# Weight sums on GpSimd, statistics in odd units and aggregation in quarters, in a two-layer window-attention and convolution kernel

## The chip, the cores and the metric

The kernel runs on one core of one Trainium2 chip. The metric is the device time of one execution in microseconds (us). Engines are named as in the profile: PE is TensorE's matmuls and PEld its weight loads, DVE is VectorE, ACT is ScalarE, POOL is GpSimd, SP is SyncE, which here issues most DMAs.

## The reference: what is computed

The input `x` is 2 images of 128 channels, 256 by 256, in float32. Two residual layers follow each other, and each first normalises its input over groups of 4 channels and a whole image:

```python
def _gn(v, G=32, eps=1e-5):
    g = v.reshape(B_, G, C_ // G, H_, W_)
    m = jnp.mean(g, axis=(2, 3, 4), keepdims=True)
    s = jnp.var(g, axis=(2, 3, 4), keepdims=True)
    return ((g - m) / jnp.sqrt(s + eps)).reshape(v.shape)
...
x = x + _L0_conv_ref(_gn(x), L0_conv_W_qkv, L0_conv_W_out, L0_conv_rel_height, L0_conv_rel_width)
x = x + _L1_conv_ref(_gn(x), L1_conv_w1, L1_conv_w3, L1_conv_w4)
```

Layer 0 is attention in windows of 8 by 8 pixels with a halo (keys from 12 by 12), 4 heads of 32, a relative position bias and a fixed mask that keeps one parity of rows and columns. Layer 1 multiplies two branches: a vertical 5-tap convolution over all channels followed by a 3-tap depthwise one, and a horizontal 3-tap product with dilation 2 into 8 channels.

What matters here is the normalisation. The mean and variance of a group need every row of the image first. So statistics of image 0 of `x` stand ahead of everything; those of image 1 of `x`, and those of layer 0's results (`y0`, `y1` in the code's names), can be gathered on the way.

## The kernel before, in words

**Work and its order.** Layer 0 handles an image in 32 strips of 8 rows, and each strip in two units (row parity `r`). Units count from 0 to 127: unit `u` is strip `k = u // 2`, parity `u % 2`; image 1 begins at unit 64. Layer 1 handles 64 strips. Inside both layers the order of instructions on every engine is the order in which the code is written (`tc.manual_schedule`); each engine works through its own queue in that order and waits on semaphores. The setup stands outside of that block.

**Setup (L220 to L247).** Image 0 comes in 32 tiles of 8 rows (`f_sx`, six buffers, L246). Each tile gets four `bn_stats` of 512 elements (L117, called by `chunk`, L115 to L119), which leave 6 numbers each in a tile of 128 × 6 = 768 per partition. Then `Norms.steps` (L121 to L158) makes mean and 1/deviation: a `bn_aggr` over the 768 (L125), a small matmul that averages over the 4 channels of a group (L128), four small DVE operations (L131 to L136), a second small matmul (L139), and a chain through ACT's square root (L142 to L156). The pool of the raw rows (`f_raw`) lies over the setup's buffers, so its first load (L283) starts when the last statistics are done.

**A unit of layer 0 (the loop at L544).** In the order of the code, and with the engines:

1. In even units: `load_rows(k + 2)` (SP, L283), then `normalise(k + 1)`: a POOL copy (L308), four DVE operations (L317) and two DVE copies (L322, L323).
2. If the unit is in `stats_at`: the next image's statistics, four `bn_stats` from the single buffer `f_sx` (DVE, L117), then the issue of the next such load (SP, L272).
3. In unit 8 alone: `weights.sums()` (L606 to L612), six DVE operations of 128x128 that prepare layer 1's weights `w1s`.
4. POOL copies (`by_place`, L331; `old_keys`, L342), which need `normalise`.
5. Matmuls of biases (L443) and scores (L459), exponentials on ACT (L468), matmuls of values (L424), whose results ACT and DVE copy out of PSUM half and half (L430).
6. Coefficients of the next strip: matmul L403, copies L412 (ACT) and L416 (DVE). Attention matmuls L484, with DVE's L490 and L491; DVE's transposes L502.
7. Queries and keys of the next unit (L349, L384, L359); statistics of the result of unit u − 1 (L117); projection (L349) and the residual sum on DVE (L518), and the store (SP, L522).

The PSUM pool `pj`, of four banks, is used in turn by L424, L403, L484, L349 and the small matmuls of `steps`, so a late copy on DVE holds up the matmul that comes four tiles later.

`stats_at` in the kernel before has units 1, 3, ..., 59 with strips 0 to 29 of image 1, and units 4 and 8 with the last two strips. `norm_at` starts the steps for `x1` in unit 61 and for `y0` in unit 69; one step is taken at each `step()` in the unit. Layer 1 takes the steps for `y1` in its strips 3 to 7 (L857); its DVE work in a strip is L691, L695, L763, L770, L776, L788 and L809, its matmuls are L704, L723, L759 and L799.

Of the kernel before, what the change touches and what calls it, by code (L numbers as in the profile page):

```python
# [19 lines left out]
P = 128  # L20
W = 256
# [83 lines left out]
class Norms:  # L105


    def __init__(self, nc, glob, small, gavg, ns):
        self.nc, self.glob, self.small, self.gavg, self.ns = nc, glob, small, gavg, ns
        self.done = {}  # L110

    def new(self, name, tag):
        return self.glob.tile([P, self.ns * 4, 6], F32, tag=tag, name=name)
# [1 line left out]
    def chunk(self, st, n, t):  # L115
        for c in range(t.shape[1] // 2):
            self.nc.vector.bn_stats(  # L117
                st[:, n + c, :], t[:, 2 * c : 2 * c + 2, :].rearrange("p a w -> p (a w)")
            )  # L119

    def steps(self, st, ps_pool, name, tag="pj"):  # L121

        nc, glob, small, gavg = self.nc, self.glob, self.small, self.gavg
        mv = small.tile([P, 2], F32, tag="mv", name=f"mv_{name}")
        nc.vector.bn_aggr(mv, st.rearrange("p n k -> p (n k)"))  # L125
        yield
        pm = ps_pool.tile([P, 512], F32, tag=tag, name=f"pm_{name}")
        nc.tensor.matmul(pm[:, 0:1], gavg, mv[:, 0:1], start=True, stop=True)  # L128
        yield
        mean = glob.tile([P, 1], F32, tag=f"mean_{name}", name=f"mean_{name}")  # L130
        nc.vector.tensor_copy(mean, pm[:, 0:1])  # L131
        d = small.tile([P, 1], F32, tag="d", name=f"d_{name}")
        nc.vector.tensor_sub(d, mv[:, 0:1], mean)
        q = small.tile([P, 1], F32, tag="q", name=f"q_{name}")
        nc.vector.tensor_mul(q, d, d)
        nc.vector.tensor_add(q, q, mv[:, 1:2])  # L136
        yield
        pv = ps_pool.tile([P, 512], F32, tag=tag, name=f"pv_{name}")
        nc.tensor.matmul(pv[:, 0:1], gavg, q, start=True, stop=True)  # L139
        yield  # L140
        v = small.tile([P, 1], F32, tag="v", name=f"v_{name}")
        nc.vector.tensor_scalar(v, pv[:, 0:1], 1e-5, None, ALU.add)  # L142
        yield
        sd = small.tile([P, 1], F32, tag="sd", name=f"sd_{name}")
        nc.scalar.activation(sd, v, AF.Sqrt)
        yield

        r0 = small.tile([P, 1], F32, tag="r0", name=f"r0_{name}")
        nc.vector.reciprocal(r0, sd)
# [16 lines left out]
def attention_fast(tc, io, x1_d, norm, st_x, st_y, tags, ends, weights):  # L166

    nc = tc.nc
    x = io["x"]
    NB, _, H, _ = x.shape  # L170
    NS = H // 8
    NU = 2 * NB * NS
    with ExitStack() as l0:
# [45 lines left out]
        with ExitStack() as setup:  # L219
            sp = setup.enter_context(tc.tile_pool(name="f_setup", bufs=6))  # L220


            wq_nat = sp.tile([P, P], F32, tag="wq_nat", name="f_wq_nat", bufs=1)
            nc.sync.dma_start(wq_nat, io["w_q"])
            relT = sp.tile([P, 2 * NREL], F32, tag="relT", name="f_relT", bufs=1)
            nc.sync.dma_start(relT, io["relT"])
            g_rel = sp.tile([P, HEADS, 2 * NREL], F32, tag="g_rel", name="f_g_rel", bufs=1)
            for h in range(HEADS):
                pg = ps_pj.tile([P, 512], F32, tag="pj", name=f"f_pg_{h}")


                nc.tensor.matmul(
                    pg[:, : 2 * NREL], wq_nat[32 * h : 32 * h + 32, :],
                    relT[32 * h : 32 * h + 32, :], start=True, stop=True,
                )
                nc.scalar.mul(g_rel[:, h, :], pg[:, : 2 * NREL], SCALE)
            for t in range(4):
                o = 11 - 2 * t
                for t1 in range(4):
                    nc.scalar.copy(wb[:, t, t1, :, 0:6], g_rel[:, :, o : o + 11 : 2])  # L240
                o = NREL + 11 - 2 * t
                for t2 in range(4):
                    nc.scalar.copy(wb[:, t2, t, :, 6:12], g_rel[:, :, o : o + 11 : 2])
            for s in range(NS):
                t = sp.tile([P, 8, W], F32, tag="sx", name=f"f_sx_0_{s}")
                nc.sync.dma_start(t, x[0, :, 8 * s : 8 * s + 8, :])  # L246
                norm.chunk(st_x[0], 4 * s, t)  # L247

        rawp = l0.enter_context(tc.tile_pool(name="f_raw", bufs=3))
        x1p = l0.enter_context(tc.tile_pool(name="f_x1", bufs=2))  # L250
# [4 lines left out]


        stats_at, norm_at = {}, {}
        for b in range(NB - 1):
            for s in range(NS - 2):
                stats_at[2 * (b * NS + s) + 1] = b + 1, s  # L260
            stats_at[2 * (b * NS + 2)] = b + 1, NS - 1
            stats_at[2 * (b * NS + 4)] = b + 1, NS - 2
            norm_at[2 * (b * NS + NS - 2) + 1] = st_x, b + 1, f"x{b + 1}"
            norm_at[2 * ((b + 1) * NS + 2) + 1] = st_y, b, f"y{b}"
        coming, sxs = sorted(stats_at), {}

        def load_next():
            if coming:
                u = coming.pop(0)
                b, s = stats_at[u]  # L270
                sxs[u] = t = rawp.tile([P, 8, W], F32, tag="sx", name=f"f_sx_{b}_{s}", bufs=1)
                nc.sync.dma_start(t, x[b, :, 8 * s : 8 * s + 8, :])  # L272

        def input_stats(u):
            b, s = stats_at[u]
            norm.chunk(st_x[b], 4 * s, sxs.pop(u))

        def load_rows(k):

            b, s = divmod(k, NS)  # L280
            t = rawp.tile([P, 10, W], F32, tag="raw", name=f"f_raw_{k}")
            n = min(10, H - 8 * s)
            nc.sync.dma_start(t[:, 0:n, :], x[b, :, 8 * s : 8 * s + n, :])  # L283
            raws[k] = t
# [245 lines left out]
        def emit(parts):  # L530
            for f in parts:
                f()

        load_rows(0)
        load_rows(1)
        load_next()
        weights.load()
        with tc.manual_schedule(engines=ORDERED):
            normalise(0)
            by_place(0, range(4))  # L540
            emit(queries(0) + keys(0))
            coefficients(0, 0)
            coefficients(0, 1)
            for u in range(NU):  # L544
                k, r = divmod(u, 2)
                b, s = divmod(k, NS)
                later, more = u + 1 < NU, k + 1 < NB * NS
                if r == 0:
                    if k + 2 < NB * NS:
                        load_rows(k + 2)  # L550
                    if more:
                        normalise(k + 1)
                if u in stats_at:
# [24 lines left out]
                turn(u)  # L578
                step()
                if later:  # L580
                    emit(queries(u + 1) + keys(u + 1))
                step()
                if u > 0:
                    result_stats(u - 1)
                project(u)
                step()
                del qs[u]
            result_stats(NU - 1)


class Weights:
# [14 lines left out]
    def sums(self):  # L606

        w = [self.w1[:, i] for i in range(5)]
        self.nc.vector.tensor_add(self.w1s[:, 0], w[1], w[3])
        self.nc.vector.tensor_scalar(self.w1s[:, 1], w[3], -1.0, None, ALU.mult)  # L610
        for i, (a, b) in enumerate(((2, 1), (4, 3), (0, 1), (2, 3))):
            self.nc.vector.tensor_sub(self.w1s[:, 2 + i], w[a], w[b])  # L612


def convolutions_fast(tc, io, x1_d, norm, st_y, out, weights, count_good):
# [859 lines left out]
```

## Time and profile before

| What | us |
|---|---|
| median of 3 runs | 3109.14 (3107.81 to 3111.26) |
| span of the profiled execution | 3104.3 |
| the median above that span | 4.8 |
| PE busy in the span | 2971.1 |
| DVE busy in the span | 2533.3 |
| DVE: one `bn_aggr` of 768 | 3.61 |
| DVE: one `bn_stats` of 512 | 0.68 (four in a row 2.46) |
| a plain unit of layer 0 | 15.47 |

How to read the profile: it is one execution. A row of a timeline is start, duration, engine, line, operation, tiles out<-in with their shape, how many were merged, and in brackets how long the engine idled before and what ended that. A row of the stretches is the stretch and its length, then busy time and instructions of PE, PEld, DVE, ACT and POOL, the granted share of TensorE's clock, the DMA engines' busy share, and GB/s. Idle time of an engine that is not the bottleneck costs nothing. Times of different rows may overlap a little, because a DVE instruction starts before the last one's record ends.

### The profile page before, as it was taken

What the parts mean: (1) busy time and instruction counts of PE and PEld (TensorE: products, weight loads), DVE (VectorE), ACT (ScalarE), POOL (GpSimd) and SP (SyncE); (2) the same over time, 40 slices, a digit from 0 to 9 for tenths busy, and PEclk for the clock granted to TensorE, in tenths of its full rate; (3) what the DMA queues carried; (4) which work ended last, traced back from release to release, by engine and by line L of the source; (5) the groups of instructions that cost most, each with busy time, mean ns of one, the idle gap of its engine ahead of it and who ended that gap; (6) DMA issues with size and microseconds to landing.
All of it is one profiled execution on the core that took longest, in us unless ns stands there. A gap on an engine that the chain in (4) does not pass through costs nothing.

```text
span 3104.3 us, 116029 instructions
## 1 busy us (share of the span) xinstructions
PE 2971.1 (96%) x52006; PEld 2248.5 (72%) x52006; DVE 2533.3 (82%) x4092; ACT 1711.4 (55%) x2673; POOL 569.0 (18%) x921
## 2 busy tenths in 40 slices
PE   0799999999999999999999999998999999999998
PEld 0688888888888888888888888884444444444443
DVE  8788888888888878777777777767999999999998
ACT  0455555555555555555555555555666665666664
POOL 2222222222222222222222222210000000000001
PEclk9999999999999999999999999999999999999999
DMA  9433333333333222222222222215788888888886
GB/s 395 160 125 128 111 115 111 115 112 115 111 115 112 84 71 87 72 86 72 88 71 87 71 88 71 84 37 168 206 217 213 221 216 213 222 215 214 217 217 167
DMA packets 137401, 434.75 MB, mean 140 GB/s; under 512 B 12993, under 2 KB 87617, under 8 KB 104385
## 3 DMA queue, kind: packets, MB, share of 16 engines
q1 hardware_dynamic: 127824, 361.18, 34.1%
q0 software_dynamic: 9072, 66.06, 11.5%
q8 instruction: 412, 6.75, 0.9%
q14 instruction: 93, 0.75, 0.1%
HBM read 284.59 MB, written 134.22 MB: 135 GB/s over the span
## 4 chain that ended last, share of the span: by engine, by line
PE 92%; DVE 2%; issue 1%; DMA 1%; ACT 0%; POOL 0%; SPq 0%; DVEq 0%; POOLq 0%; ACTq 0%
PE f_pv L424 15%; PE a_e L723 10%; PE a_o L723 10%; PE f_pq L349 9%; PE f_s L459 8%; PE f_o L484 8%; PE f_pk L349 7%; PE f_py L349 7%; PE f_pa L403 4%; PE f_s L443 4%; PE a_d L759 3%; PE b L799 2%; PE a_c L723 2%; PE g L704 2%; DVE t L788 0%
## 5 line engine op out<-in xcount | busy, mean ns | idle before, releaser
L430 DVE COPY f_vt<-f_pv 64x512 f32<-64x512 f32 x512 | 354.6, 695 | 290.7 <-ACT f_vt L430 290.5
L424 PE MATMUL f_pv<-f_wqkvT,f_xn 128*128 128x128 f32 x4096 | 491.3, 278 | 0.0
L468 ACT ACTIVATE f_p<-f_s 128x512 f32<-128x512 f32 x512 | 264.3, 603 | 404.1 <-PE f_s L459 404.1
L384 ACT ACTIVATE f_q<-f_pq,f_head 128x512 f32<-128x512 f32 x512 | 309.9, 687 | 303.0 <-PE f_pq L349 303.0
L424 PEld LDWEIGHTS f_pv<-f_wqkvT,f_xn 128*128 128x128 f32 x4096 | 466.9, 192 | 8.6
L331 POOL COPY f_xq<-f_xn 128x256 f32<-128x256 f32 x512 | 309.9, 649 | 757.9 <-DVE f_xn L317 757.9
L430 ACT COPY f_vt<-f_pv 64x512 f32<-64x512 f32 x512 | 297.4, 582 | 118.0 <-PE f_pv L424 117.8
L781 ACT ACTIVATE t<-t,w 128x1024 f32<-128x1024 f32 x128 | 147.0, 1149 | 375.2 <-DVE t L776 369.5
L788 DVE SCALAR_TENSOR_TENSOR t<-t,w,t 128x1024 f32<-128x1024 f32 x256 | 329.8, 1288 | 7.4 <-ACT t L781 1.3
L459 PEld LDWEIGHTS f_s<-f_q,f_kt 64*64 64x64 f32 x16384 | 250.6, 135 | 49.2 <-issue 49.2
L349 PE MATMUL f_pq<-f_xn,f_wq_s 128*128 128x192 f32 (+2 forms) x1520 | 277.0, 329 | 3.3 <-DVE f_xn L317 2.5
L459 PE MATMUL f_s<-f_q,f_kt 64*64 64x64 f32 x16384 | 268.1, 220 | 0.0
L484 PE MATMUL f_o<-f_vt,f_p 128*32 128x66 f32 x16384 | 264.2, 222 | 0.8 <-DVE mean_x L131 0.3
L484 PEld LDWEIGHTS f_o<-f_vt,f_p 128*32 128x32 f32 x16384 | 242.4, 110 | 10.4 <-DVE f_cf L416 1.0
L349 PE MATMUL f_pk<-f_xn,f_wqkvT 128*128 128x256 f32 x1024 | 245.2, 380 | 0.0
L349 PEld LDWEIGHTS f_pq<-f_xn,f_wq_s 128*128 128x128 f32 x1520 | 232.3, 188 | 16.9 <-issue 4.2
L349 PE MATMUL f_py<-f_ot,f_woT 128*128 128x256 f32 x1024 | 241.7, 378 | 2.3 <-DVE f_ot L502 2.3
L723 PE MATMUL a_e<-xm,w1s 128*128 128x512 f32 x512 | 240.7, 591 | 0.0
L723 PE MATMUL a_o<-xm,w1s 128*128 128x512 f32 x512 | 240.5, 590 | 0.2 <-ACT both L754 0.2
L308 POOL COPY f_xn<-f_xn 128x1280 f32<-128x1280 f32 x62 | 86.4, 1394 | 770.8 <-PE f_pv L424 770.8
L817 POOL DMA_DIRECT2D y<-f_x x63 | 54.5, 866 | 925.1 <-DVE y L809 910.1
L518 DVE TENSOR_TENSOR f_x<-f_py,f_raw 128x512 f32<-128x512 f32 x256 | 176.0, 688 | 57.9 <-PE f_py L349 50.2
(131 smaller groups left out, 4674.7 us busy)
## 6 DMA issues: line engine op xcount, KB each, us to landing
f_raw<-in_x SPq DMA_DIRECT2D x62, 1280.0 KB, 7.5
f_sx<-in_x SPq DMA_DIRECT2D x64, 1024.0 KB, 12.4
f_x<-f_x SPq DMA_DIRECT2D x128, 512.0 KB, 3.3
y<-f_x POOLq DMA_DIRECT2D x63, 1024.0 KB, 7.9
out<-y SPq DMA_DIRECT2D x63, 1024.0 KB, 4.0
raw<-f_x SPq DMA_DIRECT2D x64, 640.0 KB, 6.4
raw<-f_x SPq DMA_DIRECT2D x62, 384.0 KB, 7.7
t<-t4p SPq DMA_DIRECT2D x192, 32.0 KB, 4.3
```

The source lines that it names most:

```text
L331: nc.gpsimd.tensor_copy(xq[:, t2, half].rearrange("p t r n c e -> p r t (n c) e"), cells[:, :, 16 * half : 16 * half + 16, 1 + t2 : 9 : 4, ...
L349: nc.tensor.matmul(dst[:, 32 * lo : 32 * hi], w, moving[:, lo:hi], start=True, stop=True)
L384: nc.scalar.activation(q[:, c, :, i], pq.rearrange("p (n x) -> p n x", n=NPAIR), AF.Copy, scale=head[:, i : i + 1],)
L424: nc.tensor.matmul(pv[:, P * n : P * n + P], xn[k % 2][:, r, 4 * j + n].rearrange("p c x -> p (c x)"), wvT, start=True, stop=True,)
L430: (nc.vector.tensor_copy if c else nc.scalar.copy)(vt[rows, 4 * j : 4 * j + 4, :, c, 0:32], pv[rows].rearrange("p (n h d) -> p n h d", n=4 ...
L459: nc.tensor.matmul(sc[g][n // 8][64 * c : 64 * c + 64, n % 8].rearrange("p i x -> p (i x)"), keys_k[rows, c, 48 * n : 48 * n + 64], qs[u][ ...
L468: nc.scalar.activation(pts[u][:, g, 8 * half : 8 * half + 8].rearrange("p n i x -> p (n i x)"), sc[g][half].rearrange("p n i x -> p (n i x ...
L484: nc.tensor.matmul(po[32 * h : 32 * h + 32, n - lo], p[:, h // 2, n, h % 2], vt[:, n, h], start=True, stop=True,)
L518: nc.vector.tensor_tensor(x1[:, :, c:W:2], py.rearrange("p (m t) -> p t m", t=4), raws[k][:, r:8:2, c:W:2], ALU.add,)
L723: nc.tensor.matmul(pa[:, : n * W], w, rows, start=i == 0, stop=i == len(terms) - 1)
L781: nc.scalar.activation(t3[:, j : j + 4], t1[:, j : j + 4, :], AF.Copy, scale=w3[:, 0:1])
L788: nc.vector.scalar_tensor_tensor(t3[:, j : j + 4], t1[:, j + tap : j + tap + 4, :], w3[:, tap : tap + 1], t3[:, j : j + 4], ALU.mult, ALU.add,
```

## The change

Four edits:

- The six operations of `weights.sums()` are issued on GpSimd instead of VectorE, still in unit 8.
- Image 1's statistics are gathered in odd units only, 1 to 59. The first eight of these (1 to 15) take ten rows, five `bn_stats`, the other 22 take eight rows; units 4 and 8 have none. The buffer and the loads of the first eight grow to ten rows.
- Aggregation goes in quarters: `quarter()` runs a `bn_aggr` over 192 numbers. Three quarters are issued on the way: in setup after tiles 7, 15 and 23; at the end of units 30, 46 and 58 for `x1`; 34, 50 and 66 for `y0`; 98, 106 and 114 for `y1`. `steps` begins with the fourth.
- `steps` joins the four quarters: the first small matmul has 4 columns instead of 1, and the DVE operations between the two small matmuls are six instead of four. The mean over quarters becomes a sum and a factor 0.25.

The diff, with the unchanged lines between left out:

```diff
+    def quarter(self, st, name, i):
+        if i == 0:
+            self.mvs[name] = self.glob.tile([P, 4, 2], F32, tag=f"mv_{name}", name=f"mv_{name}")
+        self.nc.vector.bn_aggr(
+            self.mvs[name][:, i], st[:, self.ns * i : self.ns * i + self.ns].rearrange("p n k -> p (n k)")
+        )
...
-        mv = small.tile([P, 2], F32, tag="mv", name=f"mv_{name}")
-        nc.vector.bn_aggr(mv, st.rearrange("p n k -> p (n k)"))
+        self.quarter(st, name, 3)
+        mv = self.mvs[name]
...
-        nc.tensor.matmul(pm[:, 0:1], gavg, mv[:, 0:1], start=True, stop=True)
+        nc.tensor.matmul(pm[:, 0:4], gavg, mv[:, :, 0], start=True, stop=True)
...
-        nc.vector.tensor_copy(mean, pm[:, 0:1])
-        d = small.tile([P, 1], F32, tag="d", name=f"d_{name}")
-        nc.vector.tensor_sub(d, mv[:, 0:1], mean)
+        nc.vector.tensor_reduce(mean, pm[:, 0:4], AX.X, ALU.add)
+        nc.vector.tensor_scalar(mean, mean, 0.25, None, ALU.mult)
+        d = small.tile([P, 4], F32, tag="d", name=f"d_{name}")
+        nc.vector.tensor_scalar(d, mv[:, :, 0], mean, None, ALU.subtract)
+        nc.vector.tensor_mul(d, d, d)
+        nc.vector.tensor_add(d, d, mv[:, :, 1])
         q = small.tile([P, 1], F32, tag="q", name=f"q_{name}")
-        nc.vector.tensor_mul(q, d, d)
-        nc.vector.tensor_add(q, q, mv[:, 1:2])
+        nc.vector.tensor_reduce(q, d, AX.X, ALU.add)
...
-        nc.vector.tensor_scalar(v, pv[:, 0:1], 1e-5, None, ALU.add)
+        nc.vector.tensor_scalar(v, pv[:, 0:1], 0.25, 1e-5, ALU.mult, ALU.add)
...
                 norm.chunk(st_x[0], 4 * s, t)
+                if s % 8 == 7 and s < 31:
+                    norm.quarter(st_x[0], "x0", s // 8)
...
-            for s in range(NS - 2):
-                stats_at[2 * (b * NS + s) + 1] = b + 1, s
-            stats_at[2 * (b * NS + 2)] = b + 1, NS - 1
-            stats_at[2 * (b * NS + 4)] = b + 1, NS - 2
+            row = 0
+            for i in range(NS - 2):
+                n = 10 if i < 8 else 8
+                stats_at[2 * (b * NS + i) + 1] = b + 1, row, n
+                row += n
+            for i, u in enumerate((30, 46, 58)):
+                quarter_at[2 * b * NS + u] = st_x, b + 1, f"x{b + 1}", i
...
+        for b in range(NB):
+            for i, u in enumerate((34, 50, 66) if b + 1 < NB else (34, 42, 50)):
+                quarter_at[2 * b * NS + u] = st_y, b, f"y{b}", i
...
-                sxs[u] = t = rawp.tile([P, 8, W], F32, tag="sx", name=f"f_sx_{b}_{s}", bufs=1)
-                nc.sync.dma_start(t, x[b, :, 8 * s : 8 * s + 8, :])
+                t = rawp.tile([P, 10, W], F32, tag="sx", name=f"f_sx_{b}_{row}", bufs=1)
+                sxs[u] = t[:, 0:n]
+                nc.sync.dma_start(sxs[u], x[b, :, row : row + n, :])
...
                 project(u)
                 step()
+                if u in quarter_at:
+                    st, i, name, part = quarter_at[u]
+                    norm.quarter(st[i], name, part)
...
-        self.nc.vector.tensor_add(self.w1s[:, 0], w[1], w[3])
-        self.nc.vector.tensor_scalar(self.w1s[:, 1], w[3], -1.0, None, ALU.mult)
+        self.nc.gpsimd.tensor_add(self.w1s[:, 0], w[1], w[3])
+        self.nc.gpsimd.tensor_scalar(self.w1s[:, 1], w[3], -1.0, None, ALU.mult)
         for i, (a, b) in enumerate(((2, 1), (4, 3), (0, 1), (2, 3))):
-            self.nc.vector.tensor_sub(self.w1s[:, 2 + i], w[a], w[b])
+            self.nc.gpsimd.tensor_sub(self.w1s[:, 2 + i], w[a], w[b])
```

More of the change, by code (lines that the diff above doesn't have):

```diff
@@ L109, in __init__ @@
         self.nc, self.glob, self.small, self.gavg, self.ns = nc, glob, small, gavg, ns
-        self.done = {}
+        self.done, self.mvs = {}, {}
     def new(self, name, tag):
@@ L257, in attention_fast @@
         stats_at, norm_at = {}, {}
+        quarter_at = {}
         for b in range(NB - 1):
-            for s in range(NS - 2):
-                stats_at[2 * (b * NS + s) + 1] = b + 1, s
-            stats_at[2 * (b * NS + 2)] = b + 1, NS - 1
-            stats_at[2 * (b * NS + 4)] = b + 1, NS - 2
+            row = 0
[5 more added lines that the diff above has]
+                quarter_at[2 * b * NS + u] = st_x, b + 1, f"x{b + 1}", i
             norm_at[2 * (b * NS + NS - 2) + 1] = st_x, b + 1, f"x{b + 1}"
             norm_at[2 * ((b + 1) * NS + 2) + 1] = st_y, b, f"y{b}"
+        for b in range(NB):
+            for i, u in enumerate((34, 50, 66) if b + 1 < NB else (34, 42, 50)):
+                quarter_at[2 * b * NS + u] = st_y, b, f"y{b}", i
         coming, sxs = sorted(stats_at), {}
@@ L269, in load_next @@
                 u = coming.pop(0)
-                b, s = stats_at[u]
-                sxs[u] = t = rawp.tile([P, 8, W], F32, tag="sx", name=f"f_sx_{b}_{s}", bufs=1)
-                nc.sync.dma_start(t, x[b, :, 8 * s : 8 * s + 8, :])
+                b, row, n = stats_at[u]
+                t = rawp.tile([P, 10, W], F32, tag="sx", name=f"f_sx_{b}_{row}", bufs=1)
+                sxs[u] = t[:, 0:n]
+                nc.sync.dma_start(sxs[u], x[b, :, row : row + n, :])
         def input_stats(u):
-            b, s = stats_at[u]
-            norm.chunk(st_x[b], 4 * s, sxs.pop(u))
+            b, row, n = stats_at[u]
+            norm.chunk(st_x[b], row // 2, sxs.pop(u))
         def load_rows(k):
```

## The prediction, made before the result

> **What bounds the kernel now.** I read the page first: busy shares and the chain of work that ended last.
>
> ```profile
> span 3104.3 us, 116029 instructions
> PE 2971.1 (96%) x52006; PEld 2248.5 (72%) x52006; DVE 2533.3 (82%) x4092; ACT 1711.4 (55%) x2673; POOL 569.0 (18%) x921
> PE 92%; DVE 2%; issue 1%; DMA 1%; ACT 0%; POOL 0%; SPq 0%; DVEq 0%; POOLq 0%; ACTq 0%
> ```
>
> TensorE (PE) sets the time. An edit on VectorE (DVE) counts only where TensorE stood idle for it. So I looked for those places: the busy time by stretch, one stretch for each unit of layer 0 (columns: us; busy us and instructions of PE, PEld, DVE, ACT, POOL; clock; DMA).
>
> ```profile
> 173.72:190.14 16.42, 15.54 (x387) 13.93 (x381) 15.20 (x28) 8.53 (x16) 6.22 (x12) 1.00 0.53 179
> 205.60:221.07 15.47, 15.47 (x388) 13.91 (x381) 13.09 (x24) 8.53 (x16) 6.24 (x12) 1.00 0.35 123
> 236.54:257.48 20.94, 17.08 (x386) 15.43 (x380) 18.27 (x34) 8.53 (x16) 6.51 (x12) 0.92 0.42 140
> 1062.20:1079.15 16.95, 16.22 (x390) 14.40 (x384) 13.88 (x34) 10.03 (x17) 1.30 (x1) 1.00 0.10 34
> ```
>
> A plain unit lasts 15.47 us, all TensorE (second row, unit 6). Unit 4 lasts 0.95 us more, unit 8 5.47 us more, unit 61 1.48 us more (unit 69 too). The timeline of unit 8 says why.
>
> ```profile
> 237.89 2.46 DVE L117 BATCH_NORM_STATS2 st_x<-f_sx 128x6 f32<-128x512 f32 x4
> 240.27 0.27 DVE L609 TENSOR_TENSOR w1s<-w 128x128 f32<-128x128 f32 x1
> 240.47 0.63 DVE L610 TENSOR_SCALAR w1s<-w 128x128 f32<-128x128 f32 x1
> 241.02 2.34 DVE L612 TENSOR_TENSOR w1s<-w 128x128 f32<-128x128 f32 x4
> 243.39 2.52 DVE L430 COPY f_vt<-f_pv 64x512 f32<-64x512 f32 x4
> 244.23 1.72 PE L403 MATMUL f_pa<-f_xq,f_wb 128*64 128x64 f32 x32 [3.86 <-DVE f_vt L430]
> 245.88 3.03 PE L484 MATMUL f_o<-f_vt,f_p 128*32 128x66 f32 x128
> ```
>
> Statistics and weight sums stand on DVE ahead of the copies (L430) that free PSUM for L403. TensorE idles 3.86 us and then runs slowly: L403 takes 1.72 us for 1.15, L484 3.03 for 2.05. That is 3.86 + 0.57 + 0.98 = 5.41 of the 5.47.
>
> Two more places: the setup, and strip 3 of layer 1.
>
> ```profile
> 42.29 47.26 DVE L117 BATCH_NORM_STATS2 f_st_x<-f_sx 128x6 f32<-128x512 f32 x76 [0.52 <-DMA f_sx<-in_x]
> 89.59 3.62 DVE L125 BATCH_NORM_AGGREGATE mv_x<-f_st_x 128x2 f32<-128x768 f32 x1
> 89.68 0.81 SPq L283 DMA_DIRECT2D f_raw<-in_x  x2
> 96.86 3.31 DVE L317 TENSOR_SCALAR f_xn<-f_raw,mean_x,rstd_x 128x640 f32<-128x640 f32 x4
> ...
> 2168.10 3.61 DVE L125 BATCH_NORM_AGGREGATE mv_y<-st_y 128x2 f32<-128x768 f32 x1
> 2177.30 0.70 PE L723 MATMUL a_c<-sm,w1s 128*128 128x256 f32 x2 [1.31 <-DVE c L763]
> ```
>
> In setup nothing hides DVE: statistics run until 89.55, the aggregation takes 3.62, and L317 starts 7.31 after the last statistics. In layer 1 the same aggregation delays L763, and TensorE waits. Its L704 starts at 2129.08, 2144.26, 2159.74, 2174.91 and then 2192.58: that last strip lasts 17.67 for about 15.17, 2.50 too long.
>
> [...] after 3.86 us idle the unit's mean clock is 0.92; the 0.88 us stall of unit 4 leaves it at 1.00. [...] L612, beside POOL's L331, takes 0.585 us each, the same shape at L609 took 0.27. [...]
>
> **The change, part by part.** Times are of this profile.
>
> *Unit 4 loses four statistics* (2.46 us). Their DVE delay is what makes the 0.88 us stall; without them it is a unit like 6. **−0.95.**
>
> *Unit 8 loses four statistics and six sums* (2.46 + 3.12 us): it becomes a unit like 6, **−5.47**, if POOL carries the sums. In POOL's order they follow L308, which ends at 226.36, and stand ahead of L331, which starts at 237.12 after 10.76 us of waiting for DVE. L403 would start about 240.4 and the first L331 copies end at 239.6, so some 11.5 us are free. A POOL operation of 128x128 is not in the trace. [...] From L830 (2.77 us for 768) and L831 (1.70 for 256), both crowded by DVE, the line goes to 1.43 at 128. [...] They may hold DVE operations of unit 7 (two SBUF inputs): 0 to 1.5 us, I take 0. Behind them on POOL stand the f_xq and f_kt copies; `w1s` is first read in layer 1.
>
> *Statistics with ten rows in units 1 to 15:* one more operation, 0.6 us, in eight odd units. There DVE waits 1.76 us for ACT at L430 (unit 1: statistics 124.96 to 127.42, L430 at 129.18). And unit 4 shows about 1.1 us of slack behind that: its L430 came 2.04 us after ACT's copy, TensorE lost 0.95. **0.** If that cover were gone: 8 × 0.6 = 4.8. The loads on SP grow by a quarter; each has two units (31 us) to land, and 1024 KB land in 6.4.
>
> *Nine quarters inside layer 0* (units 30, 34, 46, 50, 58, 66, 98, 106, 114). A quarter reads 192 elements where the one aggregation reads 768 in 3.61. Bounds: proportional 0.90; no saving at all 3.61. The smallest DVE operations here take 0.13 to 0.16, so little of the 3.61 is fixed: I take 0.96. Each is queued behind L518 at the end of an even unit, ahead of the odd unit's statistics and their next load on SP: 0.96 against 1.76. **0.**
>
> *Final steps, units 61 and 69.* The aggregation falls to 0.96, but it was hidden: after it DVE idled 0.61 at L430. So no gain. The step after it grows from four small operations to six; their pitch is 0.195 (1069.03, 1069.23, 1069.42), so 0.39 more ahead of L490. TensorE already waits 0.38 for L490 there. **+0.39 twice, +0.78** (0 to 1.2).
>
> *Setup.* Three quarters among the statistics add 2.9. Four statistics without waits take 2.38 (unit 8: 237.89 to 240.27), in setup 2.49 a tile, with DMA at 97% and 424 GB/s (1.05 MB in 2.47): loads set the pace. DVE regains 0.11 a tile, 0.86 per eight, and the 0.52 at 42.29. I take the last statistics 0.5 later (0.2 to 2.4). Behind them DVE needs 7.31 − 2.66 + 0.39 = 5.04. But now the first f_raw load, which waits for the setup's buffers and starts 0.13 after the last statistics, is about as late: its 1.31 MB needed until about 94.2 (295 GB/s from 89.6 to 94.5)[...]: 4.7 to 5.5 after the statistics, I take 5.3. L317 at 89.55 + 0.5 + 5.3 = 95.4 for 96.86: **−1.4** (−2.1 to +0.5).
>
> *Layer 1, strip 3.* DVE is 2.65 earlier. L763 then starts at 2173.9 and TensorE needs it at about 2176: no stall, **−2.5** (−1.9 to −2.7). The two extra operations in strip 4, 0.39, fit: DVE is busy 13.8 of 15.2 in a plain strip.
>
> Sum: −0.95 − 5.47 + 0.78 − 1.4 − 2.5 = **−9.5**. Span 3104.3 becomes 3094.8. The median of the runs shown, 3109.14, lies 4.8 above the span; kept, that gives **3099.6**.
>
> **Rivals.** A: *hidden things stay late.* Setup gives nothing (+0.5, DVE-bound) and the lag in layer 1 comes back in strip 4 (−1.2): −0.95 − 5.47 + 0.78 + 0.5 − 1.2 = −6.3, 3102.8. For it: DMA and DVE are within 1% of each other in setup. Against: the 0.52 wait and the 0.11.
> B: *POOL is too slow.* At 2.5 us a sum, 15 us, f_xq is 3.5 late, and TensorE waits again in unit 8: −6.0, 3103.1. Against: no POOL operation of this size takes that; it needs over 1.9.
> C: *an aggregation costs 3.6 whatever its length.* Then setup keeps 10.8 − 2.3 = 8.5 more, plus 0.39; layer 1 gains nothing; the five quarters ahead of statistics or as tight (30, 34, 46, 50, 58) exceed 1.76 + 1.1 by 0.75, 3.7; with −6.42 and +0.78: +7.0, **slower**, 3116. It decides from a fixed part of about 2.1 of the 3.6. Against: the small operations at 0.15.
>
> **Chances.** The forecast 0.78, A 0.10, B 0.06, C 0.06. About 0.2% (6.2 us) is what a measurement of this kernel can tell from no change. Faster by over that: 0.76 from the forecast, half of A and B: 0.84. Slower by over it: most of C, 0.04. Within: 0.12. The bounds give −11.3 to −5.0, so 3097.8 to 3104.1; the runs before spread 1.5 around their median: 3096.5 to 3105.
>
> **What would show it.** Right: units 4 and 8 at 15.47, no L403 wait for L430; `w1s` on POOL between 226 and 236; an aggregation of 192 near 0.96; L317 near 95.4, held by the f_raw load; L704's strip 3 near 15.2; units 61 and 69 near 17.3. Wrong: aggregations over 2 us, POOL sums still running when f_xq is due, or new TensorE waits for L430 in the odd units.

## The result and the profile after

The changed kernel takes **3099.59 us** (median of 6 runs, 3097.64 to 3101.13) for 3108.47 (6 runs, 3106.85 to 3111.26): ratio **0.9972**, 95% interval 0.9962 to 0.9982. Predicted were 3099.6. The profiled execution is one of those six: 3099.38, and 1.8 of that lies outside its span. The page after:

```profile
span 3097.6 us, 116049 instructions
PE 2970.8 (96%) x52006; PEld 2248.3 (73%) x52006; DVE 2529.8 (82%) x4106; ACT 1710.9 (55%) x2673; POOL 571.5 (18%) x927
PE 94%; DVE 3%; DMA 1%; ACT 1%; issue 0%; SPq 0%; POOL 0%; ACTq 0%; DVEq 0%; POOLq 0%
```

TensorE is as busy as before (2971.1 then); what went is its idle time. The busy shares say little of this change, so the stretches of before are taken again, with the same columns: units 4, 8, 61 and 69, and the strip of layer 1 that had stalled. The prediction calls that one strip 3. Counted by the code's `k`, from 0, it is strip 4: the aggregation is issued in strip 3, and TensorE's wait came in the strip after it.

```profile
172.71:188.18 15.47, 15.47 (x387) 13.91 (x381) 13.07 (x24) 8.54 (x16) 6.26 (x12) 1.00 0.36 122
234.60:250.06 15.46, 15.46 (x385) 13.90 (x380) 13.08 (x24) 8.52 (x16) 6.26 (x12) 1.00 0.38 122
1054.80:1072.21 17.41, 16.30 (x390) 14.40 (x384) 12.66 (x35) 10.03 (x17) 1.30 (x1) 1.00 0.10 33
1183.15:1200.57 17.42, 16.30 (x392) 14.40 (x385) 13.07 (x36) 10.03 (x17) 1.39 (x1) 1.00 0.10 33
2170.41:2185.81 15.40, 15.40 (x58) 7.39 (x54) 14.69 (x23) 9.38 (x11) 0.86 (x1) 1.00 0.77 192
```

Units 4 and 8 are plain units now, with PE busy all the time. Units 61 and 69 are longer by 0.46 and 0.47. The strip went from 17.67 to 15.40. TensorE's waits in unit 61, before:

```profile
1068.99 0.78 PE L484 MATMUL f_o<-f_vt,f_p 128*32 128x66 f32 x40 [0.35 <-DVE mean_x L131]
1070.46 2.12 PE L349 MATMUL f_pq<-f_xn,f_wq_s 128*128 128x160 f32 x12 [0.38 <-DVE f_rc L490]
```

and after:

```profile
1061.59 0.78 PE L504 MATMUL f_o<-f_vt,f_p 128*32 128x66 f32 x40 [0.35 <-DVE f_cf L436]
1062.70 0.38 PE L149 MATMUL pv_x<-q_x,f_gavg 128*128 128x1 f32 x2 [0.33 <-DVE q_x L146]
1063.52 2.12 PE L369 MATMUL f_pq<-f_xn,f_wq_s 128*128 128x160 f32 x12 [0.44 <-DVE f_rc L510]
```

The stalled strip holds the first small matmul of the final steps in both kernels; before and after:

```profile
2184.30 0.28 PE L128 MATMUL pm_y<-mv_y,f_gavg 128*128 128x1 f32 x2
...
2177.98 0.28 PE L136 MATMUL pm_y<-mv_y,f_gavg 128*128 128x4 f32 x2
```

The timeline of the setup:

```profile
89.76 1.02 DVE L125 BATCH_NORM_AGGREGATE mv_x<-f_st_x 128x2 f32<-128x192 f32 x1
89.85 0.80 SPq L303 DMA_DIRECT2D f_raw<-in_x  x2
...
95.31 3.30 DVE L337 TENSOR_SCALAR f_xn<-f_raw,mean_x,rstd_x 128x640 f32<-128x640 f32 x4 [0.47 <-DMA f_raw<-in_x]
```

The normalisation (L337, L317 before) starts 1.55 earlier, and the load of `f_raw` now ends the last wait ahead of it. The timeline of unit 7's end and unit 8 shows the sums on their new engine:

```profile
224.49 0.45 POOL L632 TENSOR_TENSOR w1s<-w 128x128 f32<-128x128 f32 x1
224.91 0.53 POOL L633 TENSOR_SCALAR w1s<-w 128x128 f32<-128x128 f32 x1
225.42 1.69 POOL L635 TENSOR_TENSOR w1s<-w 128x128 f32<-128x128 f32 x4
229.05 0.15 DVE L527 TENSOR_SCALAR f_ok<-f_rc 128x64 f32<-128x64 f32 x1
235.21 2.48 POOL L351 COPY f_xq<-f_xn 128x256 f32<-128x256 f32 x4 [8.09 <-DVE f_xn L337]
238.36 1.15 PE L423 MATMUL f_pa<-f_xq,f_wb 128*64 128x64 f32 x32
```

Six sums take 2.62 us, POOL still waits 8.09 for DVE afterwards, and L423 (L403 before) has no wait left.

Where the span's −6.75 lies, by four marks (first L444 of unit 0, first L444 of unit 127, second L727 of layer 1, last L727):

| stretch | before | after | difference |
|---|---|---|---|
| setup and first coefficients, to unit 0 | 110.97 | 109.96 | −1.01 |
| units 0 to 126 | 1976.79 | 1971.53 | −5.26 |
| passage: unit 127 to the second L727 | 41.32 | 43.10 | **+1.78** |
| layer 1 from there to its last L727 | 945.90 | 943.67 | −2.23 |
| the rest | 29.35 | 29.32 | −0.03 |

The third row was not in the prediction, and nothing that was changed works there. The passage as one stretch, first of before:

```profile
2087.75:2129.08 41.33, 28.53 (x234) 16.56 (x227) 22.30 (x34) 15.99 (x19) 0.96 (x10) 0.83 0.38 131
```

and after:

```profile
2081.49:2124.59 43.10, 30.00 (x234) 17.38 (x227) 22.40 (x34) 15.99 (x19) 0.96 (x10) 0.76 0.37 126
```

Same instructions, but PE takes 1.47 us longer for them at a granted clock of 0.76 instead of 0.83. Inside the passage lies one stretch of half clock. Of before:

```profile
2101.43:2115.08 13.65, 6.60 (x15) 2.69 (x16) 3.79 (x3) 5.08 (x4) 0.00 (x0) 0.50 0.68 262
```

and after, with the matmuls ahead of which TensorE first idles in the passage:

```profile
2089.79 2.82 PE L369 MATMUL f_py<-f_ot,f_woT 128*128 128x256 f32 x8 [2.33 <-DVE f_ot L522]
2090.74:2111.22 20.48, 9.71 (x23) 4.64 (x22) 7.63 (x10) 5.73 (x7) 0.96 (x10) 0.50 0.58 202
```

After, it begins 9.25 us into the passage instead of 13.68, and lasts 20.48 instead of 13.65. Over the twelve profiles of this study the passage takes 43.0 to 43.7 in the seven where the half clock begins 8.3 to 9.3 us into it, and 41.2 to 42.0 in the five where it begins after 13.5 to 14.6. The two groups don't follow the edits: 42.0, 43.7 and 43.0 with one part of the change each, 43.1 and 41.75 in two profiles of the changed kernel. The profile of before drew a short one.

### The profile page after: what moved, and what is told of

The parts are those of the page before. It is cut to its first block, busy times and chain, and to the rows that moved or that the text cites. A ratio compares the mean times of both kernels' runs of the same rounds, so it can differ in the third digit from the quotient of the medians.

```text
span 3097.6 us, 116049 instructions
## 1 busy us (share of the span) xinstructions
PE 2970.8 (96%) x52006; PEld 2248.3 (73%) x52006; DVE 2529.8 (82%) x4106; ACT 1710.9 (55%) x2673; POOL 571.5 (18%) x927
## 3 DMA queue, kind: packets, MB, share of 16 engines
q8 instruction: 412, 6.75, 0.9%
## 4 chain that ended last, share of the span: by engine, by line
PE 94%; DVE 3%; DMA 1%; ACT 1%; issue 0%; SPq 0%; POOL 0%; ACTq 0%; DVEq 0%; POOLq 0%
PE f_pv L444 15%; PE a_e L746 10%; PE a_o L746 10%; PE f_pq L369 9%; PE f_s L479 8%; PE f_o L504 8%; PE f_pk L369 7%; PE f_py L369 7%; PE f_pa L423 4%; PE f_s L463 4%; PE a_d L782 3%; PE b L822 2%; PE a_c L746 2%; PE g L727 2%; DVE f_st_x L117 2%; DMA f_sx<-in_x 1%
## 5 line engine op out<-in xcount | busy, mean ns | idle before, releaser
L444 PE MATMUL f_pv<-f_wqkvT,f_xn 128*128 128x128 f32 x4096 | 491.3, 278 | 0.0
L488 ACT ACTIVATE f_p<-f_s 128x512 f32<-128x512 f32 x512 | 264.3, 603 | 404.4 <-PE f_s L479 404.4
L444 PEld LDWEIGHTS f_pv<-f_wqkvT,f_xn 128*128 128x128 f32 x4096 | 466.9, 192 | 8.6
L369 PE MATMUL f_pq<-f_xn,f_wq_s 128*128 128x192 f32 (+2 forms) x1520 | 277.1, 329 | 3.8 <-DVE f_xn L337 3.0
L504 PE MATMUL f_o<-f_vt,f_p 128*32 128x66 f32 x16384 | 263.3, 222 | 0.8 <-DVE f_cf L436 0.7
L504 PEld LDWEIGHTS f_o<-f_vt,f_p 128*32 128x32 f32 x16384 | 241.4, 110 | 10.3 <-DVE f_cf L436 1.0
L369 PE MATMUL f_pk<-f_xn,f_wqkvT 128*128 128x256 f32 x1024 | 245.2, 380 | 0.0
L369 PEld LDWEIGHTS f_pq<-f_xn,f_wq_s 128*128 128x128 f32 x1520 | 232.3, 188 | 17.5 <-issue 4.6
L369 PE MATMUL f_py<-f_ot,f_woT 128*128 128x256 f32 x1024 | 242.6, 379 | 2.3 <-DVE f_ot L522 2.3
```

Source lines behind the costliest of these rows:

```text
L369: nc.tensor.matmul(dst[:, 32 * lo : 32 * hi], w, moving[:, lo:hi], start=True, stop=True)
L444: nc.tensor.matmul(pv[:, P * n : P * n + P], xn[k % 2][:, r, 4 * j + n].rearrange("p c x -> p (c x)"), wvT, start=True, stop=True,)
L488: nc.scalar.activation(pts[u][:, g, 8 * half : 8 * half + 8].rearrange("p n i x -> p (n i x)"), sc[g][half].rearrange("p n i x -> p (n i x ...
L504: nc.tensor.matmul(po[32 * h : 32 * h + 32, n - lo], p[:, h // 2, n, h % 2], vt[:, n, h], start=True, stop=True,)
```

## The experiments

Theory: the change acts by four separate places (unit 4, unit 8, setup, the strip of layer 1), each a place where the work on DVE held TensorE up, and adds a small one in units 61 and 69. Rivals: one of the parts does nothing, or the sums on POOL only fit by luck. Single runs differ by 2 to 3 us each in the way from the first normalisation to unit 0 (14.0 to 16.7 us over the twelve profiles) and in the passage, so these runs are read by stretches; only the last two were run several times.

**The sums alone on GpSimd** (the kernel before with one edit).

```diff
-        self.nc.vector.tensor_add(self.w1s[:, 0], w[1], w[3])
+        self.nc.gpsimd.tensor_add(self.w1s[:, 0], w[1], w[3])
...
-            self.nc.vector.tensor_sub(self.w1s[:, 2 + i], w[a], w[b])
+            self.nc.gpsimd.tensor_sub(self.w1s[:, 2 + i], w[a], w[b])
```

> The kernel before with one edit: the six weight sums are issued on GpSimd. Theory (DVE delay minus a slack of about 1.1 us is what TensorE loses): unit 8 then has only the four statistics on DVE, like unit 4, so it falls from 20.94 to about 16.4 us and no half-clock stretch follows; unit 4 stays at 16.42, everything else as before. The sums take 2.7 us on GpSimd and end before 230 us. Rival[...]: unit 7 or 8 grows, unit 8 stays above 17.

Measured: 3105.12 for 3108.05 (one run each). Its unit 8:

```profile
239.50:255.97 16.47, 15.54 (x387) 13.94 (x381) 15.26 (x28) 8.55 (x16) 6.21 (x12) 1.00 0.54 178
```

That is the length of unit 4 with its statistics, as the theory has it.

**The statistics alone** (ten rows in eight odd units, none in units 4 and 8).

```diff
-            for s in range(NS - 2):
-                stats_at[2 * (b * NS + s) + 1] = b + 1, s
-            stats_at[2 * (b * NS + 2)] = b + 1, NS - 1
-            stats_at[2 * (b * NS + 4)] = b + 1, NS - 2
+            row = 0
+            for i in range(NS - 2):
+                n = 10 if i < 8 else 8
+                stats_at[2 * (b * NS + i) + 1] = b + 1, row, n
+                row += n
...
```

> The kernel before with one edit: image 1's statistics in odd units, ten rows in the first eight; sums stay on DVE, one aggregation of 768. Theory: unit 4 falls to 15.47; unit 8 keeps only the sums, some 2.6 us late at L430 minus 1.1 of slack, so about 1.4 us of stall and 16.9 us, without the slow clock. The ten-row units stay at 15.47. Rival (the two gains add up: each of the two removals is worth its share of DVE time, 2.46 and 3.12 of 5.58): unit 8 near 18.5 here and near 18.0 with the sums alone moved. Units 61 and 69 at 16.95 as before.

Measured: 3104.53 for 3108.05. Unit 4 is 15.47, units 1 to 15 keep their length, and unit 8:

```profile
236.18:253.52 17.34, 15.54 (x387) 13.93 (x380) 16.12 (x30) 8.54 (x16) 6.53 (x12) 1.00 0.33 109
```

Unit 8 is 0.4 longer than the 16.9 expected. Two things follow. Ten rows cost the odd units nothing. And in unit 8 the parts don't add: without the sums it loses 4.47 of its length, without the statistics 3.60, without both 5.48. With either one left, DVE is late by little (0.93 to 1.80 us of TensorE idle) and the clock stays at 1.00; with both, the idle time of 3.86 is followed by 3.41 us of half clock (244.58 to 248.00 in the profile of before, 0.92 in the mean of the unit), and that too is gone with either removal. The two single gains, added up (8.07), overrate the pair; a share by DVE time (2.46 of 5.58 for the statistics, which would be 2.4 us) underrates the single one.

**The quarters alone** (part of the difference to the kernel before).

```diff
-        nc.vector.bn_aggr(mv, st.rearrange("p n k -> p (n k)"))
+        self.quarter(st, name, 3)
...
+                if u in quarter_at:
+                    st, i, name, part = quarter_at[u]
+                    norm.quarter(st[i], name, part)
```

> The changed kernel with statistics back in units 4 and 8 (eight rows everywhere) and the sums back on DVE: only the aggregation in quarters is left. Theory: units 4 and 8 as before, 16.4 and 20.9; L337, the first normalisation, near 95.3 instead of 96.86 and held by the load of f_raw; units 61 and 69 at 17.4 instead of 16.95 because of the two more small operations; strip 3 of layer 1 near 15.4 instead of 17.67. Rival (setup bound by DVE): L337 at or above 96.9. Nothing else should move but the passage from layer 0 to layer 1, which was 1.8 us longer in the profile of the changed kernel: if that is chance, it falls back here.

Measured: 3106.81 for 3108.05. Normalisation at 95.61 after a wait of 0.63 for the `f_raw` load; units 4 and 8 as before (16.47, 21.04); unit 61 and the strip:

```profile
1061.62:1079.04 17.42, 16.30 (x392) 14.40 (x385) 13.03 (x35) 10.05 (x17) 1.29 (x1) 1.00 0.10 33
2177.79:2193.18 15.39, 15.39 (x58) 7.39 (x54) 14.69 (x23) 9.38 (x11) 0.86 (x1) 1.00 0.78 196
```

So the strip's gain and the loss in 61 and 69 belong to the quarters alone. The run's total says less than its places (−1.25 in setup, −2.28, +0.94): its passage took 43.0 for 41.3 in the profile of before, and units 54, 100 and 122, which the edit doesn't touch, 0.4 to 0.7 more than a plain one.

**Each quarter four times** (the changed kernel; three of four aggregations are repeats). Is a quarter free because of slack, and how much is there?

```diff
-        if i == 0:
+        if name not in self.mvs:
...
-                    norm.quarter(st[i], name, part)
+                    for _ in range(4):
+                        norm.quarter(st[i], name, part)
```

> The changed kernel with each of the nine quarters inside layer 0 aggregated four times over, 3.8 us in place of 1.0. Theory (an odd unit with statistics hides 1.76 us of idle DVE and 1.1 behind it): units 31, 35, 47, 51 and 59 grow by about 0.9 each, to 16.4; units 67, 99, 107 and 115, with no statistics, stay at 15.47. Rival (there is no such slack behind the idle time): +2.0 in the five. Rival (much more slack): nothing.

Measured: 3108.47. Units 31, 35, 47, 51 and 59 take 16.72 (+1.25 each); 67, 99, 107 and 115 stay at 15.47. Unit 31 with what precedes it:

```profile
591.13 4.18 DVE L125 BATCH_NORM_AGGREGATE mv_x<-st_x 128x2 f32<-128x192 f32 x4
...
595.23 2.41 DVE L117 BATCH_NORM_STATS2 st_x<-f_sx 128x6 f32<-128x512 f32 x4
...
597.67 2.52 DVE L450 COPY f_vt<-f_pv 64x512 f32<-64x512 f32 x4
...
598.51 1.15 PE L423 MATMUL f_pa<-f_xq,f_wb 128*64 128x64 f32 x32 [1.18 <-DVE f_vt L450]
```

Three more aggregations, 3.16 us of DVE, cost 1.25: the slack behind one quarter is 1.9. The cost is above the theory's 0.9 and below the rival's 2.0, so there is slack behind DVE's idle time, but less than reckoned. In units without the next image's statistics all of it is hidden.

**The sums five times** (the changed kernel, four of five repeats): does POOL's free window reach to the `f_xq` copies, as the prediction had it?

```diff
-                    weights.sums()
+                    for _ in range(5):
+                        weights.sums()
```

> The changed kernel with the weight sums issued five times over on GpSimd (the same values again), 30 operations. Theory: 0.44 us each makes 13.3 us, from 224.5 to about 237.8; the f_xq copies of unit 8, due at 235.2, start 2.6 us late, of which 0.8 is slack, so TensorE loses 1.5 to 2 us in unit 8 (17.2). [...] Rival (GpSimd has no part in TensorE's path here): unit 8 stays at 15.47.

Measured: 3104.83; unit 8 takes 20.73. The timeline:

```profile
229.39 0.44 POOL L633 TENSOR_TENSOR w1s<-w 128x128 f32<-128x128 f32 x1
...
231.35 3.68 DVE L527 TENSOR_SCALAR f_ok<-f_rc 128x64 f32<-128x64 f32 x1
234.96 0.52 POOL L634 TENSOR_SCALAR w1s<-w 128x128 f32<-128x128 f32 x1
235.07 0.25 DVE L528 SCALAR_TENSOR_TENSOR f_ok<-f_rc,f_ok 128x64 f32<-128x64 f32 x1
...
237.87 4.35 DVE L337 TENSOR_SCALAR f_xn<-f_raw,mean_x,rstd_x 128x512 f32<-128x512 f32 x4
...
242.28 2.48 POOL L351 COPY f_xq<-f_xn 128x256 f32<-128x256 f32 x4 [2.57 <-DVE f_xn L337]
244.03 1.47 PE L423 MATMUL f_pa<-f_xq,f_wb 128*64 128x64 f32 x32 [3.29 <-DVE f_vt L450]
245.43 3.60 PE L504 MATMUL f_o<-f_vt,f_p 128*32 128x66 f32 x128
```

My mechanism was wrong, and so was the rival: GpSimd did hold TensorE up, but not by late copies of its own. POOL ended at 239.7 and then waited 2.57 for DVE: it was DVE that was late. L527, a `tensor_scalar` from SBUF to SBUF, took 3.68 for 0.15, and four L337 took 4.35 for 2.84. Together 5.0 us; less a slack of 1.5 (unit 4 of before: 2.46 of statistics cost 0.95) to 1.9 (the quarters above) that leaves 3.1 to 3.5, and L423 waits 3.29. The slow clock comes on top (0.92 in the mean of unit 8; L423 1.47 for 1.15, L504 3.60 for 2.05).

L527 stood for longer than one GpSimd instruction: some eight of about 0.45 us, which followed each other without a gap, passed meanwhile. Why it was held is not shown. L528 behind it, with two inputs from SBUF, was not held: it took 0.25 for 0.23, beside a running sum (L634, 0.52). So in this run sums that reach L527 hold DVE: L527 starts 4.6 us after the first sum in the changed kernel, and the free window ends there, not after 11.5.

**The five sums behind the key copies** of unit 8.

```diff
-                if u == 8:
-                    weights.sums()
...
                     old_keys(u + 1)
+                if u == 8:
+                    for _ in range(5):
+                        weights.sums()
```

> The changed kernel with the sums issued five times, as in the run before, but behind the f_xq and f_kt copies of unit 8 instead of ahead of them, so that they lie beside DVE's reads of PSUM and not beside its float32 operations from SBUF to SBUF. With the sums five times ahead of the copies, DVE's L527 took 3.68 us for 0.15 and four L337 4.35 for 2.85, GpSimd then waited for DVE, and unit 8 took 20.73. Theory[...]: units 8 and 9 stay within 0.2 of 15.47 here, with the same 13.3 us of sums. Rival (GpSimd at work slows any DVE operation, or the f_kt or f_xn copies behind the sums come late): unit 8 or 9 grows by 1 us or more.

Measured: 3101.65; units 8 and 9 take 15.47.

```profile
241.21 0.44 POOL L633 TENSOR_TENSOR w1s<-w 128x128 f32<-128x128 f32 x1
...
246.02 1.31 DVE L522 STREAM_TRANSPOSE f_ot<-f_on 128x512 f32<-128x512 f32 x2
...
252.47 1.69 POOL L636 TENSOR_TENSOR w1s<-w 128x128 f32<-128x128 f32 x4
```

The same 13 us of POOL work, beside DVE's reads of PSUM, transposes and statistics, hold nobody up (units 8 and 9 at 15.47; unit 8 took 20.73 in the run above). What the sums met made the difference between these two runs, not how long they were. No `tensor_scalar` from SBUF to SBUF and no operation with two inputs from SBUF stands beside the train here, so this run says nothing of those.

**The row buffers' pool opened ahead of the setup**, so that the first `f_raw` load no longer waits for the setup's buffers.

```diff
+        rawp = l0.enter_context(tc.tile_pool(name="f_raw", bufs=3))
         with ExitStack() as setup:
...
-        rawp = l0.enter_context(tc.tile_pool(name="f_raw", bufs=3))
```

> The changed kernel with the pool of the raw rows opened ahead of the setup's, so that its first load need not wait for the setup's buffers. Theory (in the changed kernel the first normalisation waits for that load, by 0.47 us): it starts where DVE's chain ends, 5.05 us after the last statistics, 0.5 us earlier than in the changed kernel; no more, because statistics are paced by the loads. Rival (the load is not what it waits for, or the earlier load takes bandwidth from the statistics' last tiles): no gain, or the last statistics later by up to 3 us.

Measured: 3099.29. Last statistics at 89.91, and

```profile
95.08 3.31 DVE L337 TENSOR_SCALAR f_xn<-f_raw,mean_x,rstd_x 128x640 f32<-128x640 f32 x4
```

with no wait: 5.17 after the last statistics for 5.59 in the changed kernel. The load did hold the end of the setup, by 0.4 in that profile.

**The final steps spread over units.** Each small matmul goes into one step with the DVE operation that reads it, and the steps stand a unit or more apart; the statistics end two odd units earlier to make room. Shown here is only where the steps stand.

```diff
-            norm_at[2 * (b * NS + NS - 2) + 1] = st_x, b + 1, f"x{b + 1}"
-            norm_at[2 * ((b + 1) * NS + 2) + 1] = st_y, b, f"y{b}"
+            for u0, st, i, name in (
+                (2 * (b * NS + NS - 4), st_x, b + 1, f"x{b + 1}"),
+                (2 * ((b + 1) * NS + 3), st_y, b, f"y{b}"),
+            ):
+                for u, slot in ((0, 6), (1, 1), (2, 6), (3, 1), (5, 0)):
+                    norm_at[u0 + u, slot] = st, i, name
```

> The changed kernel with the final steps taken apart: statistics of image 1 end in unit 55 (ten rows in the first sixteen units), and the steps for x1 lie in units 56 to 61, those for y0 in 70 to 75, where DVE or ACT idle: the small matmul and the read of its bank right behind the value matmuls of an odd unit, the rest of the DVE work at the end of an even unit, the square root at the start of an odd unit, with one dummy exponential behind it so that the exponential's table is back before the scores. Theory (units 61 and 69 are long because DVE's small operations stand ahead of L510 and because of the two table loads on ACT): both fall from 17.41 to 15.5, units 57, 59, 71 and 73 grow by 0.3 to 0.6 for the small matmuls, unit 62 (16.4) loses up to 0.9. Sum about -3.5 us. Rival (the time is the small matmuls' own, on TensorE): the excess of 1.94 only moves to the units that now hold them. The sixteen ten-row units stay at 15.47.

Measured: 3094.94 for 3106.77. Units 61, 62 and 69 fall to 15.47 (unit 61 of the changed kernel has two table loads on ACT, 1.28 us each, at L155 and L488); units 57, 59, 71 and 73, which now hold the small matmuls, grow by 0.12 each (expected 0.3 to 0.6). So the rival is wrong: the excess did not move along. But in layer 1 a later strip, from 2225.48 to 2242.97, grows to 17.49 (15.16 in the changed kernel), since the square root and its readers came to stand in one step there:

```profile
2221.05 0.16 DVE L159 RECIPROCAL r_y<-sd_y 128x1 f32<-128x1 f32 x1 [2.95 <-ACT sd_y L154]
...
2227.68 0.70 PE L752 MATMUL a_c<-sm,w1s 128*128 128x256 f32 x2 [1.12 <-DVE c L792]
```

DVE waits 2.95 for ACT's queue, and in the next strip TensorE for DVE.

**All of it together, timed beside the changed kernel again.** The square root one strip ahead of its readers, the row buffers' pool early, the sums behind the key copies. What the square root adds to the run before:

```diff
         nc.scalar.activation(sd, v, AF.Sqrt)
...
+        yield
...
-                for _ in range({3: 1, 4: 1, 5: 1, 6: 1, 7: 1}.get(k, 0)):
+                for _ in range({3: 1, 4: 1, 5: 1, 6: 1, 7: 1, 8: 1}.get(k, 0)):
```

> The kernel after with three more edits: the final steps of each statistics spread over several units (a small matmul and the VectorE operation that reads it stand in one step, the steps one unit apart, the square root one strip ahead of its reader in layer 1), the row buffers' pool opened ahead of the setup, and the weight sums behind the key copies. My theory, that what is left of this change's subject is a wait of TensorE in units 61, 62 and 69 and a load in setup: units 61 and 69 fall from 17.41 to 15.47 (-1.94 each), unit 62 from 16.4 to 15.47 (-0.9), four units gain 0.12 for the small matmuls (+0.5), the first normalisation starts 0.3 earlier, and no strip of layer 1 is over 15.9. Sum -4.6: about 3095.0 for 3099.6. Rival: the time of these units comes back elsewhere (the start of unit 0 and the passage between the layers take it up): 3099 to 3100.

> The kernel after, unchanged, beside the other on the same chip, so that the two are compared without the difference between chips, and to see how far the profiled execution lies from the median. Expected: a ratio of 0.9971 to the kernel before (3099.6 for 3108.5), within 0.001; span of the profile 1.5 to 2.0 below its own run time; passage between the layers plus first strip between 41 and 44, other than 43.1 in the profile after, with every unit of layer 0 as in that profile within 0.1.

Measured, against one set of 11 runs of the kernel before (3108.06): all together **3094.65** (5 runs, 3091.96 to 3095.33), ratio 0.9952 (0.9939 to 0.9966); the changed kernel **3100.20** (7 runs, 3098.83 to 3101.85), ratio 0.9973 (0.9962 to 0.9985). The ranges of the two don't overlap; the gain over the changed kernel is 5.5 (expected 4.6), for the three edits together. The windows of units 61, 62 and 69 and of the strip that had stalled in the run before:

```profile
1055.32:1070.79 15.47, 15.47 (x387) 13.91 (x381) 12.11 (x23) 8.53 (x16) 1.30 (x1) 1.00 0.12 38
1070.79:1086.25 15.46, 15.46 (x386) 13.90 (x380) 11.38 (x21) 8.53 (x16) 5.62 (x10) 1.00 0.36 122
1180.79:1196.26 15.47, 15.47 (x387) 13.91 (x381) 12.10 (x24) 8.53 (x16) 1.40 (x1) 1.00 0.12 37
2227.91:2243.46 15.55, 15.45 (x56) 7.01 (x52) 14.79 (x24) 9.38 (x11) 0.86 (x1) 1.00 0.78 195
```

The second profile of the changed kernel repeats every place of the first: units 4 and 8 at 15.47, 61 and 69 at 17.42, the strip at 15.39. It differs where the two are the same: unit 0 starts at 112.46 instead of 109.96, the passage is 41.75, unit 78 is 0.96 longer, and units 38 and 46 differ by 0.27. Within 0.1 was expected of the units; why these differ stays open. The stretch from 108 to 111 us, in the first profile:

```profile
108.00:111.00 3.00, 3.00 (x138) 2.93 (x138) 2.57 (x5) 1.87 (x4) 1.20 (x2) 1.00 0.02 5
```

and in the second:

```profile
108.00:111.00 3.00, 2.98 (x112) 2.53 (x116) 2.97 (x6) 0.57 (x2) 0.17 (x1) 0.73 0.00 0
```

TensorE's granted clock once more, 0.73 for 1.00 (and 0.70 for 1.00 in the next 3 us). In the five profiles where the way from the first normalisation to unit 0 takes 16.6 to 16.7 us, a half-clock stretch of 3.41 us lies ahead of unit 0; in the seven with 14.0 to 15.5 there is none. All half-clock stretches but the last one of each profile, which ends with the profile, last 3.41, 13.65 or 20.48 us (3.41 and 13.65 in the profile of before, 20.48 in the first of the changed kernel): once, four and six times the same length. What sets these lengths is not shown. Both places follow idle time of TensorE, and the length of that alone does not tell whether the clock falls. After the 3.29 us stall with five-fold sums it fell to half, after the 1.80 us of unit 8 with the statistics alone it did not. Ahead of unit 0 TensorE idles 1.75 us in the profile of before and in the first of the changed kernel, at a clock of 1.00 up to unit 0; in the second of the changed kernel it idles about as long there (1.75 by the busy times from 105 to 111 us), and half clock follows. The first idle time of the passage, 2.33 us ahead of `f_py`, is followed within 1 us by half clock in seven of the twelve profiles and not in the other five.

## Why the prediction was right

Every term of its sum came by the mechanism that it names, at nearly its size. One baseline was misread, one bound beside the sum rested on a wrong mechanism, and the last step, from span to median, was wrong and met by luck. Term by term, in us:

| term | predicted | measured | |
|---|---|---|---|
| unit 4 | −0.95 | −0.95 | right |
| unit 8 | −5.47 | −5.48 | right |
| ten rows, nine quarters | 0 | 0 | right; slack behind a quarter 1.9 |
| units 61 and 69 | +0.78 | +0.93 | 0.46 and 0.47 for 0.39 each |
| setup, at the first normalisation | −1.4 | −1.55 | of that 1.01 reached unit 0 |
| strip of layer 1 | −2.5 | −2.27 | the baseline was 15.40, not 15.17 |
| sum | −9.5 | −9.3 | |

- **The prices.** An aggregation of 192 takes 1.01 to 1.02 (0.96 taken). A sum on POOL takes 0.45 to 0.53 and six take 2.62, for 8.6 by the line through L830 and L831 (six times 1.43). Those two stood beside DVE's L788, which took 4.02 for 2.60 itself. POOL's copies of twice the size, 128x256 (L331), had 0.65 in the mean in the profile of before.
- **Units 61 and 69.** In unit 61 TensorE's waits grew from 0.73 (0.35 and 0.38) to 1.12: 0.35, then 0.33 ahead of the second small matmul and 0.44 ahead of L369. That is the 0.39 that was reckoned for two more operations. The other 0.08 is busy time of TensorE (16.22 to 16.30), and its cause stays open. Nothing was gained from the shorter aggregation, as said.
- **Setup.** The last statistics ended 0.17 later, not 0.5: DVE caught up nearly all of three quarters behind the loads. The DVE chain behind them needs 5.17 (the run with the early load; 5.04 reckoned), the load 5.59, and the load is what came last, as said. Of the 5.3 reckoned for the load, 4.7 came from the transfers of before (1.31 MB by 94.2); the rest was the author's estimate.
- **The strip of layer 1.** The aggregation no longer delays L786 (L763 before), and the stall is gone. The prediction compared the strip with a plain one of 15.17. But it holds the first small matmul of the final steps, before and after alike, and TensorE is busy for all of its 15.40 now; so 17.67 held 2.27 of stall and not 2.50.
- **The free window of POOL, a step that was wrong.** The prediction took 11.5 us, up to the `f_xq` copies. The five-fold sums showed that DVE is held from L527 on. The real sums end 1.9 us before L527, so the term of 0 for DVE held, but with 1.9 us to spare and not 8.9; that they fitted owes something to luck. The prediction did name the danger, 0 to 1.5 us of held DVE operations, but the wrong ones: those with two SBUF inputs, like L612 beside POOL's copies (0.585 for 0.27). What was held was a `tensor_scalar` from SBUF to SBUF (3.68 for 0.15).
- **From span to median, a second wrong step.** The prediction added 4.8 to the span. Of that only 1.8 is run time outside the span (3099.38 against 3097.6). The rest is that the profiled execution of before was a short one: with 1.8 it took 3106.1, under all six runs of that kernel beside the result. After, the median stands 2.0 above its profile's span. So the addition missed by −2.8, and the span by +2.8 (3097.6 for 3094.8). Of the span's miss 1.78 is the passage; 0.4 is setup, of which 1.01 reached unit 0 for 1.4 predicted; the rest is spread over the strip, units 61 and 69 and small differences. How much of the addition's miss is a short passage is not shown, since no other execution of before was profiled. Against medians the sum was fair: −8.9 here and −7.9 in the second comparison, for −9.5. That the total met to 0.01 us is chance.

Rival A is refuted in setup and in layer 1 (no later strip took the lag back). Rival B is refuted by 0.45 a sum. Rival C is refuted by 1.02 for a quarter.

## What to carry to other kernels

Price a move by the place where the bounding engine waits, one place at a time, and check by stretches: total times of single runs hid parts of 1 to 2 us here, while most stretches of the same work agreed to 0.1 between profiles. Before work goes to GpSimd, look at what VectorE issues beside it: here 13 us beside PSUM reads, transposes and statistics cost nothing, and the same 13 us beside `tensor_scalar` from SBUF to SBUF cost 5.3 us. And a chain of tiny dependent steps (matmul, copy, square root) is better cut so that each step's result is read later: units 61, 62 and 69 lost 4.8 us together by it, and the four units that took the small matmuls gained 0.5.

## What the runs showed of the hardware that was not expected

- With five-fold sums a VectorE `tensor_scalar` of 64 elements took 3.68 us for 0.15: it stood while some eight GpSimd operations of about 0.45 us passed. Of the four `tensor_scalar` at L337 the first lost 1.5 us to the last of that train. In the kernel before, beside GpSimd copies, each of four VectorE operations with two SBUF inputs (L612) ended 0.15 us after one of those copies: 0.585 us in the mean for 0.27. Why the one waited for some eight instructions and the others did not stays open.
- The granted clock after TensorE's idle time moved the way from the first normalisation to unit 0 between 14.0 and 16.7 us, and the passage between 41.2 and 43.7, over twelve profiles: more than most single edits of this study are worth. An idle time of 2.33 us was followed within 1 us by half clock in seven of twelve profiles, and not in five.
- A `bn_aggr` takes 3.61 us for 768 elements and 1.02 for 192: an estimate from these two points is 4.5 ns an element and 0.16 us fixed.
